# Group statistics through small transfers, and stores entered one or two phases later, in a two-layer attention kernel

## Chip, cores and metric

The kernel runs on one core of a Trainium2 chip. The metric is the device time of one execution in microseconds; before the change three runs gave 3062.66, 3063.67 and 3065.93, the median is 3063.67. The engines are called TensorE (PE in the profile), VectorE (DVE), ScalarE (ACT), GpSimd (POOL) and SyncE (SP, which here only issues transfers).

## What is computed

The input x is four images of 256 channels and 64x64 points, in float32. Two layers follow each other, each of the form x + f(group norm of x):

```python
def _gn(v, G=32, eps=1e-5):            # groups of 8 channels
    g = v.reshape(B_, G, C_ // G, H_, W_)
    m = jnp.mean(g, axis=(2, 3, 4), keepdims=True)
    s = jnp.var(g, axis=(2, 3, 4), keepdims=True)
    return ((g - m) / jnp.sqrt(s + eps)).reshape(v.shape)
x = x + _L0_conv_ref(_gn(x), Wq, Wk, Wv, rel_h, rel_w)
x = x + _L1_conv_ref(_gn(x), w_qkv, b_qkv, w_pe, b_pe, w_proj, b_proj)
```

Layer 0 is attention with 8 heads of 32: q comes from a 1x1 product, k and v from a 2x2 convolution with stride 2 (1024 keys for 4096 queries), and a position term is added to k. Layer 1 is attention with 8 heads inside each of four areas of 1024 points (q, k, v from 1x1 products with bias), to which a 7x7 convolution of v, channel by channel, is added; a 1x1 projection follows.

## The kernel before

The work is eight blocks: layer 0 ("A") of the four images, then layer 1 ("B") of the four images. A block has 16 units (8 chunks of 512 queries, times 2 sets of four heads), and a unit has 8 steps, one for each 128 keys: 1024 steps in all. Steps are taken one and a half at a time; such a phase is one turn of the main loop (`while f < PHASES ...`, 683 turns). In a phase TensorE first makes the scores s (L428) of one and a half steps in three pairs of PSUM banks, ScalarE turns each pair into exponentials p (three instructions on 128x1024, L469 and L480), VectorE adds them to acc (L504) for the divisors, and TensorE multiplies the p of the phase before with v into av (L494).

Between scores and av a phase may take a piece of side work: the products for q, k, v, the values for the convolution (vals_ps), the convolution itself (conv_ps, L1048), the projection (ops), all in one PSUM bank through `ps_side`, or the divisors (den, L513). Side work is a queue of tasks (`side`); a task has two or four parts, is a generator that yields after each part, and has a due time and sometimes a condition `ready`. How many parts a phase takes (0, 1, 2 or 4) follows from `pressure()`, which looks at due times, and from `supply()`, which looks ahead up to 24 phases at the parts that will come and gives the share that may be spent now. All of this runs while the program is built: the program is a fixed list of instructions for each engine, and each engine takes its own list in order, waiting on semaphores.

What does not go through the queue is planned for a step: `at(g, j, f)` calls f at step j of unit g, at the end of the phase that reaches it. Loads, residual additions, statistics and stores are placed so.

A norm (`plan_norm`, eight of them: A0 to A3, B0 to B3) works so. VectorE gathers statistics of each channel (bn_stats, then bn_aggr into mv, L346). Then `means` multiplies the channel means with gmat, a 128x128 matrix of 1/8 in blocks of eight (gm, L351), copies the result by ScalarE (L352), and makes the deviation by three small VectorE operations (L353 to L355). `variances`, some phases later, multiplies that with gmat (gv, L359), adds eps by ScalarE (L360), and GpSimd raises it to the power -1/2 and makes shift (L363 to L368). Both go through a queue `quick`: a phase that holds one of the two products takes no other side work. For A0, which starts the kernel, they are followed by idle products (`keep_busy`). `known[key]` notes the phase in which shift and rstd are written; normalizations by ScalarE (L392) may be entered four phases later.

Values for the convolution (`plan_values`): each task computes 128 channels of one chunk, ScalarE writes it to vout (L975; two buffers, margins cleared by VectorE, L963 and L964), and SyncE stores it by four transfers, vala<-vout (L980) and vals<-vout (L988). `written[-2] + 4 <= phase[0]` keeps four phases between a task and the one that reuses its buffer. The convolution (`plan_conv`, `convolve`) uses shares of the rows of vals and of the band matrices, loaded by `load_share` (band L1029, rows L1032 in four transfers; two or three shares at a time); `chained` lets a convolution begin six phases after its shares' loads were entered. Its result cout (two buffers, shared with den_sb) is stored at L1060.

SyncE's list holds nearly all transfers in the order in which the Python code calls them. The stores xmid<-xc (L679, result of layer 0), out<-xm (L834) and those above are called right where the operation that makes their data is called, so SyncE waits there for that operation before it goes on to the loads behind. GpSimd's list holds the small operations of the norms and the transfers of the divisors (few<-den_sb, recs<-few, rb<-recs).

Of the kernel before, what the change touches and what calls it, by code (L numbers as in the profile page):

```python
# [9 lines left out]
FP = mybir.dt.float32  # L10
I32 = mybir.dt.int32
AF = mybir.ActivationFunctionType
ALU = mybir.AluOpType
AX = mybir.AxisListType

P = 128
# [44 lines left out]
def direct_path(  # L61
# [127 lines left out]

    side, quick, quick_at = deque(), deque(), [-9]
    now, last = [-1], len(BLOCKS) * UNITS * NKT

    phase = [0]

    upcoming, held = [], []

    def task(parts, f, *args, due, ready=None):

# [12 lines left out]

    def supply():

        far = 24
        comes = [0] * (far + 1)
        chained = 0
        for parts, _, started, ready, _ in side:
            if started or ready is None or ready():  # L220
                comes[0] += parts
            elif ready.__name__ == "chained":
                chained += 5
                comes[min(chained, far)] += parts
            else:
                comes[1] += parts
        for when, parts in upcoming:
            if when - phase[0] <= far:
                comes[max(when - phase[0], 1)] += parts
        total, least = 0, 4.0  # L230
        for h in range(far):
            total += comes[h]
            least = min(least, total / max(1, (h + 1) * 13 / 16))
        return least

    def choose():
# [76 lines left out]

        return ready

    def soon(f):

        if now[0] < 0:
            f()
        else:  # L320
            quick.append(f)

    stats, norms = {}, {}

# [5 lines left out]
    def keep_busy(n):  # L330
        ps = ps_pair("idle")[:, 0, :P]
        for _ in range(n):
            T.matmul(ps, lhsT=idle, rhs=idle, start=True, stop=True)

    def plan_norm(key, g, j):

        name = f"{key[0]}{key[1]}"
        made = {}

        def aggregate():  # L340
            for tag, cols in (("mv", 2), ("gmean", 1), ("dev", 1), ("gvar", 1)):
                shape = [P, CT, cols] if cols > 1 else [P, CT]
                made[tag] = pool.tile(shape, FP, tag=tag, name=f"{tag}_{name}", bufs=2)
            mv = made["mv"]
            for t in range(CT):
                V.bn_aggr(out=mv[:, t, :], in_=stats[key][:, t].rearrange("p c s -> p (c s)"))  # L346

        def means():
            mv, mean, dev = made["mv"], made["gmean"], made["dev"]
            ps = ps_side(f"gm_{name}")[:, :CT]  # L350
            T.matmul(ps, lhsT=gmat, rhs=mv[:, :, 0], start=True, stop=True)  # L351
            S.copy(mean, ps)  # L352
            V.tensor_sub(dev, mv[:, :, 0], mean)  # L353
            V.tensor_mul(dev, dev, dev)
            V.tensor_add(dev, dev, mv[:, :, 1])  # L355

        def variances():
            ps = ps_side(f"gv_{name}")[:, :CT]
            T.matmul(ps, lhsT=gmat, rhs=made["dev"], start=True, stop=True)  # L359
            S.activation(made["gvar"], ps, AF.Identity, bias=eps)  # L360
            norm = pool.tile([P, 2, CT], FP, tag="norm", name=f"norm_{name}", bufs=8)
            shift, rstd = norm[:, 0, :], norm[:, 1, :]
            G.tensor_tensor(rstd, made["gvar"], neghalf, ALU.pow)  # L363
            if key == ("A", 0):
                V.scalar_tensor_tensor(shift, made["gmean"], -1.0, rstd, ALU.mult, ALU.mult)
            else:
                G.tensor_tensor(shift, made["gmean"], rstd, ALU.mult)
                G.tensor_scalar(shift, shift, -1.0, None, ALU.mult)  # L368
            norms[key] = shift, rstd
            known[key] = phase[0] if now[0] >= 0 else -4  # L370

        def quietly(f, n):
            f()
            if key == ("A", 0):
                keep_busy(n)

        if key == ("A", 0):
            at(g - 1, 0, lambda: keep_busy(44))
        at(g, j, aggregate)
        at(g, j + (2 if g >= 0 else 1), lambda: soon(lambda: quietly(means, 4)))  # L380
        at(g, j + (6 if g >= 0 else 3), lambda: soon(lambda: quietly(variances, 10)))

    def normalize(key, dst, src, t, by_vector=False):
        while key not in norms:
            while begun():
                advance()
            quick.popleft()()
        shift, rstd = norms[key]
        if by_vector:
            V.tensor_scalar(dst, src, rstd[:, t : t + 1], shift[:, t : t + 1], ALU.mult, ALU.add)  # L390
            return
        S.activation(dst, src, AF.Identity, bias=shift[:, t : t + 1], scale=rstd[:, t : t + 1])  # L392
# [158 lines left out]
    def plan_a(b, u, prep):  # L551
# [123 lines left out]
        def store_chunk(c):  # L675
            xc = xcs.pop(c)
            for t in range(CT):
                V.bn_stats(out=stats_of(("B", b))[:, t, c, :], in_=xc[:, t, :])
            nc.sync.dma_start(xmid[b][c], xc)  # L679

        for c in range(NCH):
            g = u + 2 * c
# [22 lines left out]
    def plan_b(b, u):  # L705
# [115 lines left out]
        def project(c, to):  # L821
            cv, ps = rest[c], ps_side(f"ops_{b}_{c}_{to}")
            for t in range(CT):
                product(
                    ps, lhsT=wp_sb[:, t, to * P : (to + 1) * P], rhs=cv[:, t, :], start=(t == 0), stop=(t == CT - 1)
                )
                if t == 0:
                    yield
            xm = made_x[c]
            x_to = xm[:, to, :].rearrange("p (q f) -> p q f", f=TX)  # L830
            V.scalar_tensor_tensor(x_to, by_column(ps), bproj_sb[:, to : to + 1], x_to, ALU.add, ALU.add)  # L831
            if to == 1:
                rest.pop(c)
                nc.sync.dma_start(ov[b][:, :, c * CH : (c + 1) * CH], made_x.pop(c))  # L834

        def project_last(c):

# [105 lines left out]
                at(g + 1, 6 * k + n, lambda k=k, n=n: matrices(k, [n]))  # L943
            at(g + 1, 6 * k + 11, lambda k=k: keep(k))

    stored, convolved, written = {}, {}, [-9, -9]

    def plan_values(b, c, start):

# [10 lines left out]
        def values(t):  # L960
# [15 lines left out]
                vout[:, :, :, 1 : 1 + WW // TX], ps.rearrange("p (r x f) -> p r f x", r=RC, f=TX), AF.Identity,  # L976
                bias=bqkv_sb[:, 2, t : t + 1],
            )
            for n in range(2):
                nc.sync.dma_start(  # L980
                    vala[b][c // 2][2 * (c % 2) + n, :, 4 * t : 4 * t + 4].rearrange("c h f x -> h c (f x)"),
                    vout[:, 4 * n : 4 * n + 4].rearrange("p r f x -> p (r f x)"),
                )

            out = vout.rearrange("p r f x -> p r (f x)")
            for f in range(TX):
                at_row = (1 - f) * (XT - 1)
                nc.sync.dma_start(  # L988
                    vals[b][HALO + c * RC : HALO + (c + 1) * RC, f, t * P : (t + 1) * P, :].rearrange("r p x -> p r x"),
                    out[:, :, at_row : at_row + XT],  # L990
                )
            if t == CT - 1:
                stored[b, c] = True

        when = int(start * NKT)
        at(0, when - 5, load)
# [2 lines left out]
        for t in range(CT):  # L999
            task_at(  # L1000
                when + 7, 2, values, t, due=start + 4,
                ready=lambda: written[-2] + 4 <= phase[0] and normed("hv", b, c)(), lag=1 + 4 * t,
            )

    loaded, begun_conv = {}, set()
    shares = deque((b, k) for b in range(B) for k in range(C // TC))

    def load_share():
# [1 line left out]
        if not shares:  # L1010
            return
        b, k = shares[0]
        if b not in begun_conv or len(loaded) >= (3 if b else 2):
            return
        for c in range(NCH):
            if (b, c) not in stored:
# [23 lines left out]
    def convolve(b, n):  # L1040
        size = NY * WW // TX
        ps = ps_side(f"conv_ps_{b}_{n}")
        for k in range(2):
            band, xs, _ = loaded.pop((b, 2 * n + k))
            for i in range(2):
                for half in range(2):
                    for m in range(4):
# [4 lines left out]
                            lhsT=band[:, half].rearrange("p y (x c) -> p (y x) c", c=TC)[:, :, 4 * i + m],  # L1052
                            rhs=xs[:, half, :, 4 * i + m, : WW // TX], start=(half == 0), stop=(half == 1),
                        )
            if k == 0:
                load_share()
                yield
        out = pool.tile([P, 4, size], FP, tag="cout", name=f"cout_{b}_{n}", bufs=2)
        S.copy(out.rearrange("p i y -> p (i y)"), ps)  # L1059
        nc.sync.dma_start(  # L1060
            conv[b][16 * n : 16 * n + 16].rearrange("(i c) m y x -> (c m) i (y x)", i=4), out
        )
        load_share()
        if n == C // 16 - 1:
            convolved[b] = True
        yield

    def plan_conv(b, n, start):
# [1 line left out]
        if n == 0:  # L1070
            at(0, when - 8, lambda: begun_conv.add(b))
        def chained():
            return all(k in loaded and loaded[k][2] + 6 <= phase[0] for k in ((b, 2 * n), (b, 2 * n + 1)))

        task_at(when, 2, convolve, b, n, due=start + 2.5, ready=chained, lag=5)

# [79 lines left out]
        task(parts, g, *args, due=0.6)  # L1156
    f = step = 0
    before, credit = [], 0.0
    while f < PHASES or before or plan or side or quick or norms_left or to_add or to_divide:
        now[0], phase[0] = step, f  # L1160
        exps = scores(f) if f < PHASES else [lambda: None] * 3
        mine = []
# [24 lines left out]
        elif due and not begun():  # L1187
# [6 lines left out]
            else:  # L1194
                rb = pool.tile([P, CH], FP, tag="p", name="rb", bufs=PB)
                V.reciprocal(rb, dens[g])
                spare.extend((dens.pop(g), rb))
        elif quick and not begun() and not cut and f < PHASES and f > quick_at[0] + 2:
            quick.popleft()()
            quick_at[0] = f  # L1200
        else:
            if rate > 2:
                parts = side_parts(4)
# [11 lines left out]
        add_ready()  # L1215
        if f >= PHASES:
            side_parts(2)
        if quick and f >= PHASES:
            quick.popleft()()
        while step < -(-3 * (f + 1) // 2):  # L1220
            do(*divmod(step, NKT))
            step += 1
        for _ in range(3):
            load_share()
        if before:
# [609 lines left out]
```

## Time and profile before

| what | value |
| --- | --- |
| median of three runs | 3063.67 us |
| profiled execution, its own time | 3063.53 us |
| span of its instructions | 3061.5 us |
| granted TensorE clock, mean | 0.998 |
| TensorE, scores s L428, two groups | 541.1 and 537.1 us |
| TensorE, av L494, four groups | 451.4, 449.4, 72.4, 71.3 us |
| DMA, moved | 422.73 MB, mean 138 GB/s |
| SyncE's queue (q1), share of 16 DMA engines | 49.3% |
| GpSimd's queue (q0) | 5.1% |

The page's first part gives each engine's busy time and its share of the span; the rows of groups name line, engine, operation and tiles (out<-in) with the count, the busy time, the mean of one and the idle time in front. A float32 product of the program is recorded as two matmuls, so eight products of a side part appear as x16. In a timeline the columns are the start, the duration, and the instruction, with the idle time before it and what ended that in brackets. SPq is SyncE's sequencer: its waits are those of the list of transfers, not of TensorE.

### The profile page before, as it was taken

The numbers are of one execution on the slowest core, as the hardware profiler recorded it, in microseconds if no ns is written. First come the engines' busy times: TensorE is split into PE (matmuls) and PEld (weight loads), VectorE is DVE, ScalarE is ACT, GpSimd is POOL, SyncE is SP. The second block draws the span as 40 slices with busy tenths as digits, with TensorE's granted clock in tenths as the row PEclk, the third lists the DMA queues.
The fourth block names the chain that finished last, engine by engine and source line by source line (L and its number), as shares of the span: only waits on it lengthen the run. The fifth ranks groups of instructions, "written<-read, shape, count | busy, mean of one in ns | idle before, by whom it ended". The sixth has DMA issues, their size and how long they took to land.

```text
span 3061.5 us, 108320 instructions
## 1 busy us (share of the span) xinstructions
PE 3032.8 (99%) x47254; PEld 1280.0 (42%) x47254; DVE 2526.2 (83%) x2769; ACT 2455.9 (80%) x2988; POOL 433.8 (14%) x794
## 2 busy tenths in 40 slices
PE   9999999999999999999999999999999999999998
PEld 6444434444344444333444444444434444443332
DVE  3788988889887787878888888788878888888888
ACT  3888888888887888888888877788777787878885
POOL 0011111111111111111111111111111111111111
PEclk9999999999999999999999999999999999999999
DMA  5244533466354557777866677667755565553232
GB/s 191 51 101 98 126 92 73 109 142 165 83 140 133 143 152 175 189 161 194 204 175 162 156 176 185 152 171 178 176 127 145 144 159 143 149 139 79 50 71 62
DMA packets 644250, 422.73 MB, mean 138 GB/s; under 512 B 409740, under 2 KB 552572, under 8 KB 643768
## 3 DMA queue, kind: packets, MB, share of 16 engines
q1 hardware_dynamic: 619384, 380.11, 49.3%
q0 software_dynamic: 24384, 35.62, 5.1%
q8 instruction: 373, 6.11, 0.9%
q14 instruction: 109, 0.89, 0.1%
HBM read 317.28 MB, written 97.05 MB: 135 GB/s over the span
## 4 chain that ended last, share of the span: by engine, by line
PE 91%; DMA 3%; DVE 2%; ACT 2%; issue 2%; SPq 1%; POOL 0%; DVEq 0%; ACTq 0%; POOLq 0%
PE s L428 31%; PE av L494 26%; PE k0ps L167 4%; PE den L513 4%; PE v0ps L167 4%; PE q1ps L167 4%; PE k1ps L167 4%; PE conv_ps L1048 4%; PE q0ps L167 4%; PE ops L167 4%; PE vals_ps L167 3%; DVE acc L504 1%; ACT p L469 1%; DMA vals<-vout 1%; DMA rows<-vals 1%
## 5 line engine op out<-in xcount | busy, mean ns | idle before, releaser
L504 DVE TENSOR_TENSOR acc<-acc,p 128x1024 f32<-128x1024 f32 x1790 | 2117.4, 1220 | 382.7 <-PE av L494 285.7
L469 ACT ACTIVATE p<-s 128x1024 f32<-128x1024 f32 x1194 | 1159.8, 1025 | 419.3 <-PE s L428 407.6
L480 ACT ACTIVATE p<-s 128x1024 f32<-128x1024 f32 x598 | 619.8, 1036 | 1.5 <-DVE acc L504 0.7
L428 PE MATMUL s<-q,k_A 32*64 32x256 f32 (+1 forms) x10928 | 541.1, 494 | 4.1 <-ACT p L469 3.5
L428 PE MATMUL s<-q,k_B 32*64 32x512 f32 (+1 forms) x10912 | 537.1, 494 | 2.8 <-ACT p L469 2.4
L494 PE MATMUL av<-p,v_A 128*32 128x256 f32 (+1 forms) x4784 | 451.4, 486 | 0.0
L494 PE MATMUL av<-p,v_B 128*32 128x512 f32 (+1 forms) x4776 | 449.4, 487 | 0.0
L428 PEld LDWEIGHTS s<-q,k_B 32*64 32x64 f32 x10912 | 266.0, 130 | 325.1 <-PE s L428 60.4
L428 PEld LDWEIGHTS s<-q,k_A 32*64 32x64 f32 x10928 | 263.2, 130 | 329.1 <-PE s L428 58.5
L537 POOL DMA_DIRECT2D rb<-recs x508 | 251.4, 501 | 510.3 <-DMA recs<-few 497.9
L535 POOL DMA_DIRECT2D recs<-few x127 | 71.3, 561 | 1719.9 <-DVE sums L534 1600.3
L494 PEld LDWEIGHTS av<-p,v_B 128*32 128x32 f32 x4776 | 149.2, 110 | 264.5 <-issue 238.3
L494 PEld LDWEIGHTS av<-p,v_A 128*32 128x32 f32 x4784 | 149.5, 110 | 227.5 <-issue 186.0
L469 ACT ACTIVATE acc<-s 128x1024 f32<-128x1024 f32 x172 | 167.0, 1023 | 80.6 <-PE s L428 80.2
L513 PE MATMUL den<-acc,ones 128*32 128x512 f32 x1024 | 138.5, 605 | 0.9 <-DVE xm L831 0.9
L167 PE MATMUL ops<-cv,wp_sb 128*32 128x512 f32 x1024 | 126.6, 605 | 4.7 <-DVE xm L831 3.5
L527 POOL DMA_DIRECT2D few<-den_sb x127 | 90.5, 713 | 271.9 <-ACT den_sb L526 271.3
L167 PE MATMUL vals_ps<-hv,wqkv_sb 128*32 128x512 f32 x1024 | 124.9, 598 | 0.5 <-issue 0.5
L167 PE MATMUL q1ps<-h,wqkv_sb 128*32 128x512 f32 x1024 | 124.9, 599 | 0.0
L167 PE MATMUL k1ps<-h,wqkv_sb 128*32 128x512 f32 x1024 | 123.0, 597 | 1.7 <-ACT cout L1059 0.9
L167 PE MATMUL q0ps<-hq,wq_sb 128*32 128x512 f32 x1024 | 124.0, 597 | 0.1
L167 PE MATMUL k0ps<-taps,wkv 128*32 128x256 f32 x2048 | 123.9, 383 | 0.0
(102 smaller groups left out, 2089.5 us busy)
## 6 DMA issues: line engine op xcount, KB each, us to landing
rows<-vals SPq DMA_DIRECT2D x384, 195.9 KB
rb<-recs POOLq DMA_DIRECT2D x508, 64.0 KB, 3.6
share<-vals SPq DMA_DIRECT2D x128, 195.9 KB
vala<-vout SPq DMA_DIRECT2D x128, 144.0 KB
vals<-vout SPq DMA_DIRECT2D x128, 144.0 KB
vc<-vala SPq DMA_DIRECT2D x64, 288.0 KB
band<-mats SPq DMA_DIRECT2D x96, 176.0 KB
hq<-in_x SPq DMA_DIRECT2D x32, 512.0 KB
```

The lines of the kernel that those rows point to most:

```text
L167: T.matmul(out[cols, :], lhsT=lhsT[:, cols], rhs=rhs, start=start, stop=stop)
L428: T.matmul(out[n : n + WIDE], lhsT=unit[2]()[rows, unit[0], j * P + n : j * P + n + WIDE], rhs=unit[1]()[rows, cols], start=True, stop=True,)
L469: S.activation(p, (a, b)[n], AF.Exp, scale=SCALE)
L480: S.activation(p, c.rearrange("p b (l n) -> p b l n", l=2), AF.Exp, scale=SCALE)
L494: T.matmul(out, lhsT=v[:, j, unit[0] * P + HD * h : unit[0] * P + HD * h + HD], rhs=rhs, start=(j == 0 and not u), stop=(j == NKT - 1), sk ...
L504: V.tensor_add(to, to, p)
L513: T.matmul(dens[g][HD * h : HD * h + HD, :], lhsT=ones, rhs=p(h), start=(n == 0), stop=(n == len(sets) - 1),)
L527: G.dma_start(few[:, 0, :], den_sb[0:P:HD, :].rearrange("h (q n) -> h q n", n=CH // HD))
L535: G.dma_start(recs.rearrange("h (q n) -> (h q) n", n=CH // HD), few[:, 1, :])
L537: G.dma_start(rb[HD * h : HD * h + HD, :], recs[h : h + 1, :].to_broadcast([HD, CH]))
L1048: T.matmul(ps[HD * m : HD * m + HD, (2 * k + i) * size : (2 * k + i + 1) * size].rearrange("p (y x) -> p y x", y=NY), lhsT=band[:, half].r ...
```

## The change

1. **Norms.** For all but A0 the two products go. `gather` (one phase after bn_aggr) moves mv by two transfers from GpSimd to a tile by_group, one row for each group with its eight channels beside each other; `of_groups` takes mean and variance of the eight means and the sum of the eight variances by VectorE; `scatter` (a step later) makes shift and rstd for 32 groups by five GpSimd operations and writes them to the 128 channels by two transfers that repeat each row eight times. The queue `quick` goes.
2. **Stores.** `post(n, f)` keeps f for n phases; `hand_out()` at the end of each phase calls what is due. xmid<-xc and out<-xm are posted by two phases, the four stores of a vout and conv<-cout by one. With that, vout may be reused after five phases in place of four.
3. **Loads of shares.** `convolve` no longer calls `load_share` itself; buffers freed in this phase count as taken until the next. `chained` asks five phases in place of six.
4. **Look-ahead.** `supply` counts when tasks of values will be allowed by their spacing, counts 6 in place of 5 phases for each convolution in a chain, ends its view at the last phase, and divides by 14/16 in place of 13/16 of the phases.

```diff
     def supply():
-        far = 24
+        far = max(1, min(24, PHASES - phase[0]))
         comes = [0] * (far + 1)
-        chained = 0
+        chained, kept = 0, written[-2:]
         for parts, _, started, ready, _ in side:
-            if started or ready is None or ready():
+            if started or ready is None:
+                comes[0] += parts
+            elif ready.__name__ == "spaced":
+                kept.append(max(phase[0] + (0 if ready() or kept[0] + 5 > phase[0] else 1), kept[-2] + 5))
+                comes[min(kept[-1] - phase[0], far)] += parts
+            elif ready():
                 comes[0] += parts
             elif ready.__name__ == "chained":
-                chained += 5
+                chained += 6
...
-            least = min(least, total / max(1, (h + 1) * 13 / 16))
+            least = min(least, total / max(1, (h + 1) * 14 / 16))
...
+    def post(n, f):
         if now[0] < 0:
             f()
         else:
-            quick.append(f)
+            posts.append((phase[0] + n, f))
+    def hand_out():
+        due = [f for at, f in posts if at <= phase[0]]
+        posts[:] = [(at, f) for at, f in posts if at > phase[0]]
+        for f in due:
+            f()
...
+        def gather():
+            by_group = made["by_group"] = pool.tile([CT * NG, 8, 2], FP, tag="by_group", name=f"by_group_{name}", bufs=1)
+            for t in range(CT):
+                G.dma_start(by_group[t * NG : (t + 1) * NG], made["mv"][:, t, :])
+        def of_groups():
...
+            V.bn_stats(out=made["spread"], in_=by_group[:, :, 0])
+            V.bn_aggr(out=made["of_means"], in_=made["spread"])
+            V.tensor_reduce(made["within"], by_group[:, :, 1], AX.X, ALU.add)
+        def scatter():
...
+            G.tensor_scalar(within, within, 0.125, EPS, ALU.mult, ALU.add)
+            G.tensor_tensor(within, within, of_means[:, 1:2], ALU.add)
+            G.tensor_tensor(rstd, within, neghalf[: CT * NG, 0:1], ALU.pow)
+            G.tensor_tensor(shift, of_means[:, 0:1], rstd, ALU.mult)
+            G.tensor_scalar(shift, shift, -1.0, None, ALU.mult)
+            norm = pool.tile([P, CT, 2], FP, tag="norm", name=f"norm_{name}", bufs=4)
+            for t in range(CT):
+                G.dma_start(norm[:, t, :], scale[t * NG : (t + 1) * NG].unsqueeze(1).to_broadcast([NG, 8, 2]))
             known[key] = phase[0] if now[0] >= 0 else -4
...
-        at(g, j + (2 if g >= 0 else 1), lambda: soon(lambda: quietly(means, 4)))
-        at(g, j + (6 if g >= 0 else 3), lambda: soon(lambda: quietly(variances, 10)))
+            for n, f in (((1, gather), (7, of_groups), (8, scatter)) if g >= 0 else ((1, gather), (2, of_groups), (3, scatter))):
+                at(g, j + n, f)
...
-            nc.sync.dma_start(xmid[b][c], xc)
+            post(2, lambda: nc.sync.dma_start(xmid[b][c], xc))
...
-                nc.sync.dma_start(ov[b][:, :, c * CH : (c + 1) * CH], made_x.pop(c))
+                made_x.pop(c)
+                post(2, lambda: nc.sync.dma_start(ov[b][:, :, c * CH : (c + 1) * CH], xm))
...
+            post(1, store)
+        def spaced():
+            return written[-2] + 5 <= phase[0] and normed("hv", b, c)()
...
-                ready=lambda: written[-2] + 4 <= phase[0] and normed("hv", b, c)(), lag=1 + 4 * t,
+                ready=spaced, lag=1 + 4 * t,
...
-        if b not in begun_conv or len(loaded) >= (3 if b else 2):
+        if b not in begun_conv or len(loaded) + sum(f == phase[0] for f in freed) >= (3 if b else 2):
...
+            freed.append(phase[0])
             if k == 0:
-                load_share()
                 yield
...
-        load_share()
-        if n == C // 16 - 1:
-            convolved[b] = True
+        post(1, store)
...
-            return all(k in loaded and loaded[k][2] + 6 <= phase[0] for k in ((b, 2 * n), (b, 2 * n + 1)))
+            return all(k in loaded and loaded[k][2] + 5 <= phase[0] for k in ((b, 2 * n), (b, 2 * n + 1)))
...
-        elif quick and not begun() and not cut and f < PHASES and f > quick_at[0] + 2:
-            quick.popleft()()
-            quick_at[0] = f
...
+        hand_out()
         for _ in range(3):
             load_share()
```

## The prediction

> **What bounds the kernel now.** I read the page's busy times and its chain first: they say which engine the sum has to be made on.
>
> ```profile
> PE 3032.8 (99%) x47254; PEld 1280.0 (42%) x47254; DVE 2526.2 (83%) x2769; ACT 2455.9 (80%) x2988; POOL 433.8 (14%) x794
> PE 91%; DMA 3%; DVE 2%; ACT 2%; issue 2%; SPq 1%; POOL 0%; DVEq 0%; ACTq 0%; POOLq 0%
> ```
>
> TensorE is busy all the time and is 91% of the chain. Its products for attention, projections and convolution are the same before and after, so only two things can move the time: how well the side work is spread over the phases, and the few stalls. The next view is the timeline of TensorE alone around a phase with a norm product, and around a phase with no side work.
>
> ```profile
> 1245.46 1.47 PE L494 MATMUL av<-p,v_A 128*32 128x256 f32 x16
> 1246.86 1.55 PE L428 MATMUL s<-q,k_A 32*64 32x256 f32 x32
> 1248.34 0.38 PE L351 MATMUL gm_B<-mv_B,gmat 128*128 128x2 f32 x2
> 1248.65 1.50 PE L494 MATMUL av<-p,v_A 128*32 128x512 f32 x16
> 1250.10 2.00 PE L428 MATMUL s<-q,k_A 32*64 32x256 f32 x32
> 1252.03 1.92 PE L167 MATMUL vals_ps<-hv,wqkv_sb 128*32 128x512 f32 x16
> 1253.77 1.47 PE L494 MATMUL av<-p,v_A 128*32 128x256 f32 x16
> ```
>
> ```profile
> 1289.51 1.54 PE L428 MATMUL s<-q,k_A 32*64 32x256 f32 x32
> 1290.99 1.50 PE L494 MATMUL av<-p,v_A 128*32 128x512 f32 x16
> 1292.68 2.00 PE L428 MATMUL s<-q,k_A 32*64 32x256 f32 x32 [0.20 <-ACT p L469]
> 1294.62 1.92 PE L167 MATMUL vals_ps<-hv,wqkv_sb 128*32 128x512 f32 x16
> ```
>
> A phase runs from one group of scores (s) to the next. With a full side product it takes 4.62 us (1.48 scores, 1.74 side, 1.40 av). The one at 1246.86 holds only the norm product and takes 3.24; the empty one at 1289.51 takes 3.17, although scores and av alone are 2.88: ScalarE's three exponentials (1.03 each) do not fit in less. The phase after either is longer too: its scores stretch from 1.55 to 2.00, because ScalarE is still behind. So a phase without real side work costs about 0.3 itself and 0.46 in the next.
>
> The third view is the waits on the tile vout, the fourth SyncE's own waits.
>
> ```profile
>   DMA vals<-vout: 10.3, 4
> ```
>
> ```profile
> SPq L1029 <- PE conv_ps L1048: 308.4, 41, 19.3
> SPq L834 <- DVE xm L831: 264.1, 18, 40.2
> SPq L679 <- DVE xc L673: 207.3, 15, 27.3
> SPq L980 <- DVE vout L964: 109.0, 20, 17.6
> ```
>
> SyncE stands 889 us at the four lines that the change touches, but the 10.3 us are where late stores reach a computing engine: vout's next user cannot begin until the old contents are stored.
>
> **The sum by phases.** From the order of TensorE's instructions in both programs I counted the 682 full phases by their side work and by whether the phase before was light (empty, or a norm product alone); from the trace I took the median time of each kind. Phase 0 is taken apart below.
>
> - empty, after a loaded phase: 25 before, 31 after, 3.17 us: +19.0
> - empty, after a light one: 5, 1, at 3.36: -13.4
> - norm product alone: 12, 0, at 3.22: -38.6
> - one part of side work, after loaded: 201, 207, at 3.76: +22.6
> - one part, after light: 16, 22, at 4.22: +25.3
> - two parts, after loaded: 396, 406, at 4.62: +46.2
> - two parts, after light: 18, 9, at 5.07: -45.7
> - four parts: after loaded 5, 4 at 6.36: -6.4; after light 2, 0 at 7.01: -14.0
>
> The sum is -5.0 us. This already contains two parts of output projection (two times 0.88 us) that the new order brings forward from the tail. Phase 0 was 6.01 us (with a variance product and its wait for ScalarE inside); without it, scores plus four parts are 4.95: -1.06. Together -6.0. Light phases fall from 42 to 32: that is what removing 14 small products and the new look-ahead are worth on the bounding engine, and not the 0.26 us of the products.
>
> **The tail.** From the last scores (3033.4) to the end it is VectorE's order that counts: addition of the last rows, reciprocal (3.33 us), projection, output. The two parts taken out were under VectorE's waits there. One addition to xm (0.75) moves ahead of the last row's normalization, and the store of xm_6, posted two phases later, still goes out last. Along VectorE's rows I get its issue at 3056.2 instead of 3055.74. I take +0.4.
>
> **The norms through transfers.** For seven of the eight norms two products, two ScalarE copies (0.19 and 0.28) and three VectorE operations (0.16 each) go. In their place come two gathers, two small VectorE statistics and a reduction on 32 partitions, five small POOL operations and two scatters. VectorE's additions lie between 0.2 (the reduce on few takes 0.19) and 0.34 (aggregation) each: about 0.5 more in seven places, under additions that have 383 us of idle time. ScalarE saves 3 us in all, already inside the phase times.
>
> The wait is what could cost. Gather and statistics are four phases apart in the program's order, scatter and the first use of shift and rstd at least four: 4 times 4.4, about 17 us each. No transfer of this shape runs before. The nearest rows are few<-den_sb, 0.71 us of issue and 4.3 to landing, and recs<-few, 0.56 and 3.8. A gather is then about 2 times 0.7 plus 4.3, under 6 us. POOL in front may stand up to 7.2 us at a rb<-recs: 13, inside 17. The scatter has POOL's five operations (norm_B's 1.2 for a scale, 1.4 for the power, 0.5 for a product: 4.9), issue and landing 5.7, and the same wait: up to 18 against 17. If covered it costs nothing; at worst 1 to 2 us on ScalarE in the three norms used after exactly four phases. VectorE waiting would hold all acc additions behind it, ScalarE waiting all exponentials. I take 0 and keep +5 for the range. Rows rb behind these on POOL have five phases (22 us) for about 10: also 0.
>
> One rule speaks against this part. The Trainium skill (DMA: Bandwidth & Descriptors, sections "Anatomy of one DMA — SWDGE (gpsimd) path" and "Measured") fits about 2.0 us of fixed cost to each DMA and calls transfers under 64 KB dominated by descriptors; these move 1 KB. By the rule 28 of them are at least 56 us for 14 products of 0.26 us, a bad trade; by the rows it would be worse, 28 times 4. Both would hold if anybody stood waiting. The rows show who does: rb<-recs waits 497.9 us for landings in 127 cases, and VectorE behind it 1.6 us in one. Latency that the order spans with phases is free, and I keep 0.
>
> **The stores handed over later.** vala and vals (four transfers per value tile) and conv move one phase on, xmid and out two. On SyncE's queue they pass the loads issued meanwhile: hq, xc and hv with 0.4 to 3.3 us of issue, and the shares, about 3.4 us each (band 0.4, rows 3.0). In turn the loads no longer stand behind SyncE's waits for VectorE and TensorE. Share loads are entered a phase later but needed five phases on instead of six: the same time. The spacing of values is five phases instead of four, so a vout store keeps its four phases of order, and gains up to one phase (4.6) where SyncE was not loaded.
>
> What is at stake is what the phase medians leave over. The phases measure 2961.4, my kinds give 2943.0: 18.4 us of other stalls. By looking at each stretched phase, about 8 belong to transfers, all between 1236 and 1507, where values and convolution run together: 1.4 at 1241 (vals<-vout landed 11.5 us after its issue), 1.5 at 1359, and 5 between 1381 and 1402 (hq late by 2.0, vout by 4.7). The rest are waits for VectorE's xm, 0.5 each, and ScalarE's lag, which I leave. The bounds: all 8 gone, or 8 more. In 24 places the new order reuses a vout three to five phases after its store, against 16 before (three to four: 13 against 8). I take half the stalls gone, -4: the late hq no longer sits behind a share, and the real gap grows where SyncE has room, but in the dense stretch two shares (7 to 11 us) pass in front of the store.
>
> **Sum.** -6.0 (phases) +0.4 (tail) +0 (norm waits) -4 (stores) = -9.6. The profiled execution took 3063.53 us, span 3061.5 and 2.0 around it; the median of the three runs is 3063.67, the same within 0.2. So 3054.
>
> **Rivals.**
> 1. Stores half relieved, as above: 3054. Chance 0.40.
> 2. SyncE is limited by issuing in that stretch (1217 to 1260 is issue after issue), so the later hand-over shifts stalls and removes none: 3063.5-6.0+0.4, about 3058. For it: vals<-vout itself needs 5.3 us of issue there. Against: hq's delay came from what stood in front. Chance 0.27.
> 3. All transfer stalls go, and some of VectorE's with the split projections: 3063.5-6-8, about 3049. Chance 0.18.
> 4. The other side, slower: a vout store behind two shares lands after VectorE's clearing of the next vout (L963), which holds the acc additions, then the exponentials, then TensorE. The trace has its price: 1.4 to 1.7 us per case, up to 5 when cases follow each other. It decides when a store goes out more than one phase (4.6 us) later than now. With the 13 close reuses at 1.5 it is +20 less 6: 3077. Against it: most of the 64 tiles lie outside the dense stretch. Chance 0.15.
>
> That the change does not do what it says is excluded for the products, since they are gone from the order; for the stores it is rival 2.
>
> About 0.2% (6.1 us) is what a measurement of this kernel can tell from no change. Faster by more: rivals 1 and 3 and a little of 2, 0.62; within: most of 2, 0.24; slower: 0.14. The range from 3046 (all stalls gone and a little of VectorE's) to 3066 leaves out most of rival 4 and the edge of 3.
>
> **What would show it.** Right: TensorE's empty phases at 3.17 us, 32 of them, no L351 inside the loop; the sum of SyncE's waits at the value, residual and output stores far under 580 us; vout's wait for its store under 10.3 us; no wait for by_group on VectorE or norm on ScalarE above 1 us. Wrong: VectorE idle before vout for more than 10 us in all, TensorE waiting for conv_ps's rows or band (0.4 us now), or a stall at a first normalized tile.

## The result, and the profile after

The kernel after takes 3098.02 us (median of 4 runs, 3095.28 to 3099.4), before 3063.16 in the same comparison: a ratio of 1.011, interval 1.0098 to 1.0123. It is slower by 1.1%; the prediction was 3054. The profiled execution took 3095.28 us, its span is 3093.5.

The page's busy times and its chain, for the kernel after:

```profile
PE 3027.7 (98%) x47226; PEld 1282.2 (41%) x47226; DVE 2525.3 (82%) x2769; ACT 2454.7 (79%) x2974; POOL 465.5 (15%) x836
PE 91%; ACT 2%; DMA 2%; DVE 2%; issue 2%; SPq 1%; POOL 0%; ACTq 0%; DVEq 0%; POOLq 0%
```

```profile
PEclk9999999999999999899999999999999999999999
```

TensorE is busy for 5 us less than before in a span that is 32 us longer, so it stands idle. Neither the shares nor the chain say where. The clock row points to one slice, the 17th (1237 to 1315 us). The view by stretches of 100 us (busy time of each engine, then granted clock, DMA share, GB/s) confirms it for after:

```profile
1100.00:1200.00 100.00, 99.80 (x1684) 44.93 (x1677) 81.81 (x90) 84.04 (x104) 12.96 (x24) 1.00 0.53 133
1200.00:1300.00 100.00, 73.99 (x1040) 28.96 (x1029) 54.55 (x71) 60.85 (x75) 15.14 (x26) 0.85 0.61 147
1300.00:1400.00 100.00, 99.60 (x1558) 41.31 (x1560) 82.83 (x98) 83.62 (x102) 14.61 (x27) 1.00 0.74 168
```

Between 1200 and 1300 us TensorE, ScalarE and VectorE lose a quarter to a third of their busy time together, while transfers are no denser than in the next stretch (DMA share 0.61 against 0.74): somebody waits for one late thing. The waits between 1240 and 1285 us name it (total, times, longest):

```profile
DVE vout L997 <- DMA vals<-vout: 22.3, 2, 16.2
ACT vout L1009 <- DMA vals<-vout: 21.7, 2, 18.5
PEld conv_ps L1089 <- ACT vout L1009: 18.0, 1, 18.0
PE conv_ps L1089 <- ACT vout L1009: 17.6, 1, 17.6
```

VectorE cannot clear the next vout and ScalarE cannot fill it, since its old contents are not stored; TensorE then waits for the eviction that ScalarE has not made. The view of the tile vout has the total of this wait over the span; it was 10.3 us in 4 cases before:

```profile
  DMA vals<-vout: 60.2, 8
```

Why the store is late is seen on SyncE, in its timeline around the stall and its waits over the span:

```profile
1235.60 1.97 SPq L108 DMA_DIRECT2D hq<-in_x  x1
1256.38 0.34 SPq L989 DMA_DIRECT2D hv<-xmid  x1
1256.81 0.39 SPq L1103 DMA_DIRECT2D conv<-cout  x1
1257.25 0.45 SPq L1070 DMA_DIRECT2D band<-mats  x1
1257.76 2.23 SPq L1073 DMA_DIRECT2D rows<-vals  x4
1260.03 0.38 SPq L1070 DMA_DIRECT2D band<-mats  x1
1260.63 3.06 SPq L1073 DMA_DIRECT2D rows<-vals  x4
1264.28 1.40 SPq L1016 DMA_DIRECT2D vala<-vout  x2
1266.20 4.40 SPq L1024 DMA_DIRECT2D vals<-vout  x2
```

```profile
SPq L1103 <- ACT cout L1100: 299.5, 39, 21.2
SPq L869 <- DVE xm L865: 278.7, 16, 37.6
SPq L713 <- DVE xc L707: 142.0, 12, 19.9
SPq L1016 <- DVE vout L998: 74.2, 17, 9.7
SPq L989 <- PE vals_ps L167: 39.6, 2, 20.8
```

SyncE issues nothing from 1237.6 to 1256.4. Next in its list is the load of hv for image 1, chunk 7 (L989), which waits for a chunk buffer that TensorE's products of values still read. Behind it stand a conv store, two shares and the store of vout. The store reaches the queue at 1264.3, and ScalarE has the buffer 11.6 us later. In before the same load was entered behind the shares and behind a store of vout, and the last products that read its buffer's old contents stood four phases earlier. Before's row for this wait is the only one of its kind there, and belongs to this load:

```profile
SPq L955 <- PE vals_ps L167: 2.9, 1, 2.9
```

Now it is 39.6 us in two cases (20.8 ending at 1196.8 us, 18.8 here). The four largest waits add up to 794 us against 889 (the first was at the shares' load and is now at the convolution's store), and the three stores that the prediction put at 580 us to 495. The last row shown is the one that hurts.

To see what each part did, I split each span the same way: the start up to the first scores, phase 0, the other 681 phases at the median of their kind in before, what phases take over these medians (the stalls), and the tail from the last scores on. Each row is one execution; those of one kernel lie 2 to 11 us apart in all, so that a few us between two rows say nothing by themselves.

| us | start | phase 0 | phases at medians | stalls | tail | span |
|---|---|---|---|---|---|---|
| before | 72.1 | 6.0 | 2937.1 | 18.3 | 28.1 | 3061.5 |
| after | 69.1 | 5.1 | 2932.1 | 56.1 | 31.0 | 3093.5 |
| e1 vout at once | 69.0 | 5.1 | 2932.6 | 56.1 | 32.7 | 3095.4 |
| e2 xmid, out at once | 70.2 | 5.1 | 2932.1 | 54.2 | 31.6 | 3093.2 |
| e3 norms only | 70.1 | 5.1 | 2928.6 | 20.6 | 30.3 | 3054.8 |
| e4 hv later | 69.2 | 5.1 | 2932.2 | 28.4 | 32.4 | 3067.2 |
| e5 before, vout later | 70.2 | 6.0 | 2937.1 | 45.0 | 28.3 | 3086.6 |
| e6 order of after, all at once | 70.5 | 5.1 | 2932.2 | 17.9 | 33.8 | 3059.4 |
| e7 norms, hv later | 69.4 | 5.1 | 2928.5 | 37.5 | 30.2 | 3070.6 |
| e8 as e7, xmid later | 69.1 | 5.1 | 2928.5 | 35.7 | 29.1 | 3067.5 |
| e9 norms, spacing five | 69.5 | 5.1 | 2928.9 | 11.3 | 29.7 | 3044.5 |
| e10 milder look-ahead | 70.1 | 5.1 | 2930.7 | 13.3 | 33.7 | 3052.9 |
| e11 one hv later | 69.0 | 5.1 | 2932.2 | 39.5 | 32.7 | 3078.4 |

Between before and after the stalls alone account for +37.9 us; everything else sums to -5.9. Of the 56.1, phases 261 to 271 (1203 to 1282 us) hold 31.7, the one at 1257.5 us 20.2 by itself. A second group, 9.1 us in phases 145 to 153 around 695 us, begins with ScalarE waiting for a late hv:

```profile
ACT hv L426 <- DMA hv<-xmid: 7.4, 1, 7.4
```

### The profile page after: what moved, and what is told of

It is laid out like the page before. It is cut to its first block, busy times and chain, and to the rows that moved or that the text cites. A ratio compares the mean times of both kernels' runs of the same rounds, so it can differ in the third digit from the quotient of the medians.

```text
span 3093.5 us, 108337 instructions
## 1 busy us (share of the span) xinstructions
PE 3027.7 (98%) x47226; PEld 1282.2 (41%) x47226; DVE 2525.3 (82%) x2769; ACT 2454.7 (79%) x2974; POOL 465.5 (15%) x836
## 4 chain that ended last, share of the span: by engine, by line
PE 91%; ACT 2%; DMA 2%; DVE 2%; issue 2%; SPq 1%; POOL 0%; ACTq 0%; DVEq 0%; POOLq 0%
PE s L462 31%; PE av L528 26%; PE conv_ps L1089 4%; PE den L547 4%; PE q1ps L167 4%; PE v0ps L167 4%; PE k1ps L167 4%; PE q0ps L167 4%; PE k0ps L167 4%; PE ops L167 3%; PE vals_ps L167 3%; ACT p L503 1%; DVE acc L538 1%; DMA vals<-vout 1%; DMA rows<-vals 0%
```

## Experiments

Theory 1: a load of hv that waits for a chunk buffer stands in SyncE's list in front of transfers that other engines wait for. Theory 2: the stores are simply too late, with no such wait needed (rival 4 of the prediction, with two shares in front). Comparisons are with before on the same chip.

**e1: the stores of vout at once.** After, but:

```diff
-            post(1, store)
+            store()
```

> The changed kernel, but the four stores of a vout are entered in SyncE's list at once, as before; their spacing of five phases and all else stay. Theory 1 (a vout store now stands behind a load of hv that itself waits for a buffer which the values task behind vout must free): the stretches at 1203 (6.1 and 2.0), 1239 (1.9 and 1.5) and 1258 (20.2 us) go, 31.7 in all: 3098 becomes about 3066. Theory 2 (the store is late because it is entered a phase later and stands behind the shares' loads): the same, about 3066. Theory 3 (the norms through transfers make the stalls): 3095 or more.

Measured 3101.81 us, ratio 1.0143 (1.0126 to 1.016): as slow as after. Both theories expected 3066 and missed. The trace shows the stall with another victim, 13.9 us in the phase at 1247.8 us. Waits between 1190 and 1300 us:

```profile
PE conv_ps L1089 <- DMA rows<-vals: 15.8, 8, 6.2
DVE vout L997 <- DMA vals<-vout: 10.3, 1, 10.3
```

vout's stores now pass the load of hv, but the conv store and the shares, which the change also hands over a phase later, still stand behind it; so TensorE waits for rows. What is common to both kernels is the load in front, which waits for its buffer as in after. SyncE's waits between 1235 and 1300 us:

```profile
SPq L989 <- PE vals_ps L167: 14.7, 1, 14.7
```

This run is not a clean trial of the place of the stores alone: ScalarE and VectorE do not have quite after's list in it, and stalls of 4 to 6 us stand at 1209, 1289 and 1375 us too.

**e4: the load of hv itself one phase later.** After, with all its postponed stores and shares:

```diff
-            nc.sync.dma_start(made["h"], xmid[b][c])
+            post(1, lambda: nc.sync.dma_start(made["h"], xmid[b][c]))
```

> The changed kernel, with the load of hv in plan_values also kept back one phase, so that it stands behind the vout stores of the phase before in SyncE's list. The lists of TensorE, ScalarE, VectorE and GpSimd are the same as in the changed kernel, and the stores stay a phase later and behind the shares' loads. Theory 1: the 31.7 us go as well, about 3066 to 3070. Theory 2: nothing changes, 3095 to 3098.

Measured 3068.91 us, ratio 1.0033 (1.0022 to 1.0045): of the 32 us over before in the span, 26 are gone. The view of the tile vout in this run:

```profile
  DMA vals<-vout: 6.8, 4
```

TensorE, ScalarE and VectorE have the list of after, instruction by instruction; only the place of the hv loads on SyncE differs. Theory 2 falls for these 26 us: the stores are as postponed as in after, and vout waits 6.8 us instead of 60.2. What remains is mainly the group at 695 us, grown from 9.1 to 12.7.

**e11: one single load.** After, but only the load seen in the timeline above is moved, by one phase:

```diff
+            if (b, c) == (1, 7):
+                post(1, lambda: nc.sync.dma_start(made["h"], xmid[b][c]))
+            else:
+                nc.sync.dma_start(made["h"], xmid[b][c])
```

> The kernel after with one single load moved: that of hv for image 1, chunk 7, is handed to SyncE one phase later (266 in place of 265), behind the convolution's store, both shares and one store of vout. Every other instruction of every engine keeps its place. Theory 1: this load's wait for a chunk buffer is what holds the 20.2 us stall at 1257 us; it goes, and the 6 to 8 us at 1203 us (hv of 255 and 260) and the 9 us at 695 us stay: 3074 to 3080. If the stall has another cause, such as the later shares or the postponed stores themselves, it stays: 3093 to 3100.

Measured 3079.93 us, ratio 1.0065 (1.0051 to 1.008), against 1.011 for after. One instruction in another place is worth 15 us of span; the stall at its place goes from 20.2 to 7.7. It is not gone, as Theory 1 had it. The waits between 1240 and 1285 us:

```profile
ACT vout L1012 <- DMA vals<-vout: 6.7, 1, 6.7
PE conv_ps L1092 <- ACT vout L1012: 5.3, 1, 5.3
```

```profile
1245.41 2.29 SPq L1019 DMA_DIRECT2D vala<-vout  x2
1248.15 6.62 SPq L1027 DMA_DIRECT2D vals<-vout  x2
1254.88 2.69 SPq L990 DMA_DIRECT2D hv<-xmid  x1
```

ScalarE begins at 1260.0, when the vals store of 1248.15 has landed, and that one stands in front of the load now. Ahead of it SyncE issues the convolution's store and two shares (1235.9 to 1244.5). So this rest is Theory 2's.

**e5: the old kernel with vout's stores one phase later, nothing else.**

```diff
-            for n in range(2):
-                nc.sync.dma_start(vala...)
...
+            post(1, store)
```

> The kernel before with one part of the change alone: the stores of vout are handed to SyncE one phase later, everything else (norms by products, spacing of four phases, shares and all other stores) as before. The order of work on TensorE differs from before in 6 of 683 phases. Theory 1 (a load of hv that waits for a chunk buffer stands in front of the store that the next clearing of vout waits for): in phases 255, 260 and 265 the load of hv now stands in front of vout's stores, and before it stood behind them; with two or three such places a stall of 5 to 20 us each time the chunk buffer comes late, so 3070 to 3085. Theory 2 (the postponement by itself costs one phase of slack and no more, as the prediction had it): vout's waits grow from some 10 us by at most 5, 3060 to 3066.

Measured 3086.13 us, ratio 1.0072 (1.0058 to 1.0087). This one part makes the old kernel slower by more than half of what the whole change does. The number is 1 us above what theory 1 expected, but the trace gives it another cause. The largest stalls are 6.8 us at 699 (a late hv, as in after, though the products stand where before has them), 8.0 at 1247, 8.3 at 1396 and 9.1 at 1452, and SyncE waits at no load of hv in front of the last three; the only long wait there (8.8 us, ending at 1189.2) holds up nobody. What stands in front of the store at 1396 us is this, with SyncE idle for under 1 us at a time:

```profile
1378.03 0.37 SPq L1048 DMA_DIRECT2D share<-mats  x1
1378.45 2.14 SPq L1051 DMA_DIRECT2D share<-vals  x4
1380.69 0.79 SPq L1079 DMA_DIRECT2D conv<-cout  x1
1381.58 0.64 SPq L1048 DMA_DIRECT2D band<-mats  x1
1382.52 3.65 SPq L1051 DMA_DIRECT2D rows<-vals  x4
1386.88 0.35 SPq L970 DMA_DIRECT2D hv<-xmid  x1
1387.61 2.33 SPq L997 DMA_DIRECT2D vala<-vout  x2
1390.91 5.81 SPq L1005 DMA_DIRECT2D vals<-vout  x2
```

That is rival 4 as it was written: one phase later, two shares and a conv store go first, and TensorE waits 5.3 us for conv_ps behind the eviction of vout. The same stand in front at 1247 and 1452 us. So there are two prices. With four phases between the clearings of vout, as here, a phase of delay alone costs 8 to 9 us at each of three dense places; with five, as in after, that is nearly paid for (vout waits 6.8 us in all in e4; one case of 7.7 us is left in e11), and the wait at hv is what costs most.

**e6: after's order, but all stores at once and the shares inside the convolution.** Before with the new norms, look-ahead and spacing:

```diff
-                ready=lambda: written[-2] + 4 <= phase[0] and normed("hv", b, c)(), lag=1 + 4 * t,
+                ready=spaced, lag=1 + 4 * t,
```

and `supply` as in after; TensorE, ScalarE and VectorE then have exactly after's list.

> The kernel before with the new norms and the new look-ahead and spacing, but every store handed to SyncE at once and the shares loaded inside the convolution as before. TensorE, ScalarE and VectorE have exactly the list of the kernel after; only SyncE's list differs. Theory 1 (the big stall comes from the loads of hv in front of stores and shares): hv stands behind vout's stores and behind the shares again, so the group at phases 261 to 271 shrinks from 31.7 us to under 8. The group at phases 145 to 153 (9.1 us in after) comes from the order of the products of values, two phases later than before, which frees the chunk buffers later: it stays, 8 to 14 us. Together 3062 to 3068. Rival: that group is SyncE's doing as well, and goes: 3053 to 3058. Rival: the spacing itself costs the big stall: 3085 to 3100.

Measured 3063.28 us, ratio 1.0004 (0.9996 to 1.0012): like before. Its view of the tile vout:

```profile
  DMA vals<-vout: 0.4, 1
```

In its SyncE waits the loads of hv still stand for up to 12.9 us:

```profile
SPq L980 <- PE vals_ps L167: 18.5, 2, 12.9
```

The 12.9 us are at the load that waited 20.8 in after; the one of image 1, chunk 7 waits 5.7 (1235.6 to 1241.4). The new order makes it wait: the last products of image 1, chunk 3, which free its buffer, stand in phase 270 and not in 266, while the load keeps its place in phase 265. But with the stores in front of it the wait costs nothing, and vout's waits are gone. It takes both, the long wait and the stores behind it, to make the stall. The group at 695 us falls from 9.1 to 3.9 us, less than I expected to stay: the order seems to make part of it and the later hand-over the rest (e5 has the hand-over alone, and 6.8 us). Against e4 (1.0033) e6 also shows that the postponed stores and shares bring nothing even with hv out of their way.

**e2: the stores of xmid and out at once.** After with both `post(2, ...)` replaced by the plain transfers.

> The changed kernel, but the stores of xmid and of the result are entered at once, not two phases later; the lists of the computing engines stay the same. Theory 1: the vout stalls (31.7 us) remain; if holding the chunk buffers two phases longer is what made hv late at 695 (5.4, 1.7, 1.2 and 0.8 us), these go: 3089, with the large stalls. Theory 2: 3098, unchanged. If the two-phase stores are the whole cause: about 3063.

Measured 3094.75 us, ratio 1.0111 (1.0094 to 1.0128): the same as after. These stores cost nothing and gain nothing, and the late hv at 695 us is not theirs (10.1 us in the group there, against 9.1).

**e3: the norms through transfers alone.** Before with the new plan_norm and without the loop that waits for a norm in normalize.

> The kernel before with the norms through transfers alone; stores, loads of shares and look-ahead as before. By the phase medians of before its list gives 2928.4 in place of 2937 to 2944, 8 us less. Theories 1 and 2: 3053 to 3058, since no store moves. Theory 3: the waits of the norms cost what the products gave: 3063 or more, with VectorE waiting for by_group or ScalarE for norm.

Measured 3055.9 us (20 runs), ratio 0.9988 (0.9981 to 0.9995): a small gain. The phases at medians give back 8.5 us, more than with the look-ahead (5.0), and the stalls are 20.6, of which 5.2 are one wait for vout at 1286 us.

**e7 and e8: e3 with a later hv, and with a later xmid too.** The edit of e4 in e3; e8 adds `post(2, ...)` around the store of xmid.

> The kernel before with the new norms, and the load of hv handed to SyncE one phase later; no other store or load is moved, and the order of the other engines is that of the run with the norms alone (3055.9). If a load of hv that waits in front of stores is what costs, then also the remaining stall of that run (5.2 us at 1286 us, conv_ps behind ACT vout) may shrink, though there no hv stood directly in front of the store: 3051 to 3057. If a later hv only makes its normalization late, as at 695 us in the kernel after: 3060 to 3070.

> As the run with norms and a later hv, and the store of xmid is handed to SyncE two phases later too. The remaining stall at 1286 us in the run with the norms alone comes while xmid's store (issued at 1284.5 us) lies between the stores of two vouts; two phases later it lies behind the next one. If xmid's bytes in front of vout's are that stall: 1 to 5 us less than the run without, about 3050. If not, the same as without within 2 us; if the chunk buffer that xmid frees is needed two phases earlier, 3058 to 3065.

Measured 3072.31 us, ratio 1.0032 (1.0021 to 1.0044), and 3072.4, 1.0033 (1.002 to 1.0046): both slower than e3 by 0.4% and above what was expected of e7, and the stall at 1286 us grew from 5.2 to 10.2 and 8.6 instead of shrinking. Where hv stood behind the stores already, moving it only puts it in front of, or behind, something else. At 1432 to 1457 us it falls behind two shares, is issued at 1457.2 (in e3 its load goes out at 1434.8, before them), and ScalarE waits for it. Waits between 1455 and 1475 us in e7:

```profile
ACT hv L427 <- DMA hv<-xmid: 5.6, 1, 5.6
DVE acc L539 <- ACT p L515: 4.8, 1, 4.8
PE s L463 <- ACT p L504: 4.7, 1, 4.7
```

So "hv later" is no remedy as such; it paid in after because there it took a wait out from in front of the stores. Whether xmid's bytes delay vout stays unshown; posting it later changed nothing measurable.

**e9: e3 with spacing five, and nothing else.**

```diff
-                ready=lambda: written[-2] + 4 <= phase[0] and normed("hv", b, c)(), lag=1 + 4 * t,
+                ready=lambda: written[-2] + 5 <= phase[0] and normed("hv", b, c)(), lag=1 + 4 * t,
```

> The run with the norms alone (3055.9), and five phases instead of four between the clearings of vout; look-ahead, stores and loads as before. Theory 1: the spacing is the part of the change that does take vout's waits away (they were 0.4 us in all with the order of after and SyncE's list as before), and it costs nothing by itself; but here the load of hv of phase 265 happens to stand in front of the stores of vouts 266 and 267, as the products are now made a phase later than that load. If that place alone is enough: one stall of 5 to 20 us near 1240 us, 3060 to 3072. If the buffer it waits for is free by phase 267, the stall is under 2 us: 3050 to 3055.

Measured 3049.22 us, ratio 0.9967 (0.9956 to 0.9979): faster than before and after, the best of the study. No engine waits for a store of vout any more, and the stalls fall to 11.3 us. Here too a load of hv stands in front of two vouts' stores at phase 265, and SyncE waits only 3.8 us at it (1218.4 to 1222.2), because the buffer's last products stand in phase 267 and not in 270. The place in the list is harmful only where the wait is long.

**e10: e6 with 13 sixteenths in the look-ahead instead of 14.**

> The new norms, spacing five and the new look-ahead, but with 13 sixteenths of a part per phase as before in place of 14; all stores at once and shares inside the convolution as before. The products of values of phases 136 and 137 stand where they stood before, not at 137 and 138. If the later chunk buffers at 640 to 700 us came from that order, the group at phases 145 to 153 (9.1 us in after, 3.9 with after's order and all stores at once) is gone, under 1 us; vout's waits stay under 2 us, as hv stands behind the stores at 265: 3050 to 3056. If the group stays, 3057 to 3063.

Measured 3060.67 us, ratio 1.0003 (0.9995 to 1.0012). The group at 695 us is gone, as expected if it came from placing the products at phases 137 and 138, and the profiled execution (3054.68 us) lies in the expected range; but 10 of the 12 runs lie 4 to 10 us above that one, and the median is outside the range. What these runs do otherwise the one trace does not show; that stays open. In its trace the tail is 33.7 us, 4 more than e9's.

## Why the prediction was wrong

**Phases, -6.0: right.** The phases at medians went from 2937.1 to 2932.1 and phase 0 from 6.01 to 5.07: -5.0 and -0.94. The first of these repeats the prediction's own count. That it holds is seen from the medians of after, which are those of before within 0.01 us for each kind, and from e6: with after's order and no new stalls, all phases together take 2955.2 us, 6.2 less than in before.

**Norms through transfers, 0: right.** In the loop no VectorE instruction waits for by_group and no ScalarE one for norm. The gathers land 2.3 to 7.6 us after issue (medians 4.4 in layer 0, 4.6 in layer 1, where I took 4.3); POOL's busy time rises from 433.8 to 465.5. The one wait lies before the loop, where gather and statistics follow each other closely, and it is inside the start:

```profile
DVE spread_A L393 <- DMA by_group_A<-mv_A: 5.0, 1, 5.0
```

The rule on small transfers would have made this part a loss; e3 shows a gain of 0.12%, since nobody stands waiting.

**Tail, +0.4: +3.0.** I counted VectorE's rows up to the last issue. That comes no later after the last scores than before (21.4 us against 22.3). But the last three stores of out leave within 1.6 us instead of 2.6, and the end comes 9.6 us after the last issue, against 5.8. Every run with the new look-ahead has a tail of 31.0 to 33.8, every run without it one of 28.1 to 30.3, so the term belongs to the order of the last work. Why the stores land so much later the runs don't show.

**Start.** It was not in the sum and moved by -2.9. e5 has the old norms and 70.2, so most of it is the spread between executions (69.0 to 70.5 in all later ones). In before's trace the granted clock is 0.91 in the first 40 us, in after's 1.00.

**Stores later, -4: +37.9. This is the step that failed.** It said that the stores pass "hq, xc and hv with 0.4 to 3.3 us of issue", and concluded that a vout store "keeps its four phases of order, and gains up to one phase". I priced what the store is moved past by its issue time and put the wait of such a load at nothing. A load's price on a list that is worked off in order is its issue and its wait: this hv waits 18.8 us for a chunk buffer, another 20.8, and SyncE issues nothing meanwhile. (The Trainium skill, "DMA: Bandwidth & Descriptors", section "Anatomy of one DMA — SWDGE (gpsimd) path", says of all DMA engines that a transfer's wait takes place on the issuing engine before dispatch. The trace agrees: the gap of 18.8 us on SyncE is such a wait.) The distance in phases between a store and the next use of its tile says nothing as long as another instruction of the list can stop between. e11 (one load moved, 15 us), e4 (all of them moved, 26 us) and e6 (nothing postponed, no stall) show it, and e5 that even without the wait the delay is not free where the spacing is four. The prediction's own sign of being wrong came true: VectorE idle before vout for 31.9 us, against 6.5 in before. The needed facts were in the order of the two programs: the line of SyncE's list where hv changes places with the stores, and which products have to be done before that load can start.

**Rival 4** named the right victim, the clearing of vout, and the right side. Its mechanism (shares in front) is real, but worth 8 to 9 us per case with spacing four (e5), not 1.4 to 1.7, and it was the smaller part of what after suffered from: in e11 it is left with 7.7 of the 20.2 us at 1257 us. The rest comes from the load, whose wait closes on itself. Phase 270's products free hv's buffer; the eviction of these products needs a vout whose store stands behind hv; and conv_ps of phase 271 needs that eviction. SyncE restarts only when TensorE has reached the end of phase 270, and then TensorE waits for all that SyncE has left undone.

## What to carry to other kernels

When a transfer is moved in an in-order queue, list for each load that it is moved behind what that load waits for and when that is free, and not only how long its issue takes; a wait on buffer reuse in front of a store can be longer than all slack given by the order. When one part of a change fails, try the others alone: norms through transfers and the spacing of five (e9) were worth 0.33%, hidden under a loss three times as large.

## What the runs showed of the hardware beyond that

A stall costs more than the gap in it. In after TensorE runs at half the granted clock for some microseconds behind each of its three longest gaps in the loop (5.3 us ending at 704.7, 6.3 at 1211.9, 17.6 at 1276.7), and once where gaps of 0.75 and 1.18 us follow each other (1241.0 to 1243.6). Stretches of after (same columns as above):

```profile
701.60:708.30 6.70, 3.59 (x36) 1.28 (x40) 4.36 (x7) 6.28 (x8) 0.00 (x0) 0.50 0.82 230
1244.30:1247.60 3.30, 3.30 (x28) 0.96 (x28) 1.46 (x2) 3.29 (x6) 1.98 (x4) 0.50 0.24 70
1259.10:1261.20 2.10, 0.00 (x0) 0.00 (x0) 0.66 (x1) 0.00 (x0) 0.00 (x0) 1.00 0.94 325
1262.00:1277.00 15.00, 0.34 (x8) 0.34 (x12) 1.04 (x3) 1.10 (x2) 0.00 (x0) 0.50 0.63 163
1277.00:1283.00 6.00, 6.00 (x100) 3.89 (x96) 5.86 (x7) 3.61 (x5) 0.00 (x0) 0.60 0.79 173
```

The work after the long gap shows it, in TensorE's timeline of after: the convolution part takes 3.65 us where it takes 1.93 at 1161.3, and av 2.31 instead of 1.50.

```profile
1276.65 3.65 PE L1089 MATMUL conv_ps<-rows,band 88*32 88x128 f32 x64 [17.57 <-ACT vout L1009]
1280.08 2.31 PE L528 MATMUL av<-p,v_A 128*32 128x512 f32 x16
1282.32 1.55 PE L462 MATMUL s<-q,k_A 32*64 32x256 f32 x32
```

By these two rows the half clock added about 2.5 us to this stall, an estimate; with the gap of 17.6 that makes up its 20.2. The Trainium skill ("TensorE: Matmul & The Clock Gate", Part 1, "What's actually happening") says that the clock is halved after an idle window of some 3.4 us and restored after as long a busy one. The rows agree in the order of size only. TensorE's last product ended at 1259.1, and the clock was full up to 1261.2 and half from 1262: it fell 2 to 3 us after that product. At 1244.3 it was at half though TensorE had stood still for no more than 1.18 us at a time. As to the second, the mean of 0.60 over the 6 us from 1277 means that the half clock lasted some 5 us after the restart at 1276.65, an estimate from that row.
